# Strassen products of a two-layer graph network: sums read between the products, and quarter blocks for the output projection

## The chip, the cores and the metric

The kernel runs on one core of one Trainium2 chip. TensorE (PE) multiplies matrices, VectorE (DVE) and ScalarE (ACT) work elementwise and can read PE's results in PSUM, GpSimd (POOL) works elementwise on SBUF alone, and SyncE (SP) issues most of the DMAs. Each engine works through its own queue in order, and waits for others by semaphores. The metric is the device time of one execution in microseconds, the median of several runs. All data are 32-bit floats.

## The reference

x is 64 batches of 256 tokens with 512 features. Two layers follow each other, each with a layer norm and a ReLU ahead of it and a residual around it:

```
h = relu(layernorm(x));  x = x + (adj @ h) @ W0 + b0
h = relu(layernorm(x));  q, k, v = h @ Wq + bq, h @ Wk + bk, h @ Wv + bv     # 8 heads of 64
a = softmax(q k^T / 8 + (1 - adj) * -1e9)
x = x + (a v) @ Wo + bo
```

## The kernel before, in words

**Tiling.** The batches are worked in NG = 32 groups of two. All groups go through layer 0 first (`layer0`, L643), which leaves the residual and the turned hidden state in HBM; then all go through layer 1. Layer 1 of a group is: queries and keys (`queries_keys`, L755), scores (`score`, L825, in two halves of the heads, qd), values (`values`, L780), attention (`attend`, L860) and the output projection (`post`, L800). The loop at L970 interleaves neighbours: attend(g, 0), score(g, 1), queries and keys of g + 1, attend(g, 1), score(g + 1, 0), values of g + 1, output projection of g.

**Projections.** Every projection is a product of a 512x512 weight with 512 columns (two batches of 256 tokens), cut into 2x2 blocks of 256, and computed by Winograd's form of Strassen's algorithm: seven block products instead of eight. Their operands are sums of blocks: s1 to s4 of the weight, made once (`weight_sums`, L405), and t1 to t4 of the data (`Halves.sums`, L433), made by POOL for each group. `product` (L439) writes one block product into a PSUM bank with four matmuls, each 128 columns of weights by 256. There are eight banks; `bank` (L246) takes the one that has been free longest, and `give` returns it. Some products add up in the same bank: `project` (L447) writes a11 b11 into bank a, has it read, adds s2 t2 on top, has it read again, adds s3 t3, and so on; it uses four banks a, b, c and d. ACT (for q, k and v) or DVE (layer 0 and o, onto the residual x) reads a bank, and DVE adds the other parts (`add`, L608).

**Quarter size.** From group FIRST2 = 4 on, q, k and v use `project2` (L561). There four of the seven products (a11 b11, s1 t1, s2 t2, s3 t3) are done as before, and the three that are used in one place only (a12 b21, s4 b22, a22 t4) are cut once more into seven products of quarter blocks, one 128x128x128 matmul each (`product2`, L534). Of these seven, three go straight to their place in the bank `own`, and the four common ones (a11 b11, s2 t2, s3 t3, s1 t1) lie side by side in four quarters of another bank, `shared`. After all seven DVE adds each to the quarters that need it (`finish2`, L547): widths 512, 512, 384, 256 and 128 or 256. The output projection uses `project` for all groups.

**Order.** The order of the instructions is written by hand. PE's work is emitted in steps (a `yield` after each product), and after each step `tick` (L263) emits what was put off with `after(delay, ...)`: subtractions of the scores' bound (POOL, L846), exponents (ACT, L851), sums over keys (POOL, L858), divisions (DVE, L901), data sums. Each engine then runs its own instructions in this order.

**The end.** In the last group there is nothing left to project ahead, so the output projection of the group before (`run(post(g - 1))`, L989) stands between score and attend; then the last attention, and the last output projection (L1001), into which a check on the softmax's denominators (L1004 to L1011) is put.

Of the kernel before, what the change touches and what calls it, by code (L numbers as in the profile page):

```python
# [13 lines left out]
P = 128  # L14
# [184 lines left out]
def kernel(  # L199
# [247 lines left out]
    def project(s, halves, by_token, name, read, finish, in_place=False):  # L447

        def new(n):
            return bank([P, 2, N], f"{name}{n}")

        def p1():
            o["a"] = new("a")
            product(o["a"], s, "a11", halves, "b11", by_token, stop=False)
            o["u1"] = read(o["a"], 1)

        def p2():
            pb = new("b")  # L460
            product(pb, s, "a12", halves, "b21", by_token)
            finish(pb, o["u1"], 0, 0)
            give(pb)

        def p3():
            product(o["c"], s, "s4", halves, "b22", by_token, start=False)
            finish(o["c"], o["u2"], 0, 1)
            give(o["c"])

        def p4():  # L470
            pd = new("d")
            product(pd, s, "a22", halves, "t4", by_token)
            finish(pd, o.get("u3"), 1, 0)
            give(pd)

        def p5():
            o["c"] = new("c")
            product(o["c"], s, "s1", halves, "t1", by_token, stop=False)
            o["c22"] = read(o["c"], 0)

        def p6():
            product(o["a"], s, "s2", halves, "t2", by_token, start=False, stop=False)
            o["u2"] = read(o["a"], 2)

        def p7():
            product(o["a"], s, "s3", halves, "t3", by_token, start=False)
            o["u3"] = read(o["a"], 3)
            finish(o["a"], o["c22"], 1, 1)
            give(o["a"])

        o = {}
        for step in (p1, p5, p2, p6, p4, p7, p3) if in_place else (p1, p2, p6, p5, p7, p4, p3):
            step()
            yield

# [5 lines left out]
    FIRST2 = 4  # L501
    W2, spare = {}, []

    def block_sums(n):

        todo = []
        for a in ONCE:
            w = W[n][a]
            def part(i, j):
                return w[:, j, i * P:(i + 1) * P]  # L510
            s1, s2, s3, s4 = (spare.pop(0) for _ in range(4))
            W2[n, a] = dict(a11=part(0, 0), a12=part(0, 1), a22=part(1, 1), s1=s1, s2=s2, s3=s3, s4=s4)
            for o, p, q, op in ((s1, part(1, 0), part(1, 1), ALU.add), (s2, s1, part(0, 0), ALU.subtract),
                                (s3, part(0, 0), part(1, 0), ALU.subtract), (s4, part(0, 1), s2, ALU.subtract)):
                todo.append((nc.gpsimd.tensor_tensor, o, p, q, op))
        return todo
# [17 lines left out]
    def product2(own, shared, s, x, by_token, fresh):  # L534

        q = own.rearrange("p m (n k) -> p (m n) k", k=P)
        c11, c12, c21, c22 = (q[:, i, :] for i in ((0, 2, 1, 3) if by_token else (0, 1, 2, 3)))
        for o, a, b, start in ((shared[:, 0, :], "a11", "b11", True), (shared[:, 1, :], "s2", "t2", False),
                               (shared[:, 2, :], "s3", "t3", False),
                               (c22 if fresh else shared[:, 3, :], "s1", "t1", fresh),  # L540
                               (c11, "a12", "b21", False), (c12, "s4", "b22", False), (c21, "a22", "t4", False)):
            lhs, rhs = s[a], x.operand(b)
            if by_token:
                lhs, rhs = rhs, lhs
            nc.tensor.matmul(o, lhs, rhs, start=start, stop=True, skip_group_check=True)

    def finish2(o, own, shared, u, by_token, fresh):  # L547

        def quarters(t):
            return t.rearrange("p m (n k) -> p (m n) k", k=P)  # L550

        def spread(i, n):
            return shared[:, i:i + 1, :].to_broadcast([P, n, P])
        q = quarters(o)
        lower = q[:, 1::2, :] if by_token else q[:, 2:4, :]
        right = q[:, 2:4, :] if by_token else q[:, 1::2, :]
        return [(o, own, u), (q, spread(0, 4), q), (q[:, 1:4, :], spread(1, 3), q[:, 1:4, :]),
                (lower, spread(2, 2), lower),
                (right[:, 0, :], quarters(own)[:, 3, :], right[:, 0, :]) if fresh else (right, spread(3, 2), right)]

    def project2(n, halves, blocks, by_token, name, read, target):  # L561

        s = W[n]

        def new(i):
            return bank([P, 2, N], f"{name}{i}")

        def once(own, a, i, k, u, fresh):
            shared = bank([P, 4, P], f"{name}r")
            product2(own, shared, W2[n, a], blocks[ONCE[a]], by_token, fresh)  # L570
            return own, shared, finish2(target(i, k), own, shared, u, by_token, fresh)

        def finish_all(*products):
            for ops in zip(*(ops for _, _, ops in products)):
                for op in ops:
                    add(*op)
            for own, shared, _ in products:
                give(own)
                give(shared)

        pa = new("a")
        product(pa, s, "a11", halves, "b11", by_token, stop=False)
        u1 = read(pa, 1)
        yield
        pc = new("c")
        product(pc, s, "s1", halves, "t1", by_token, stop=False)
        c22 = read(pc, 0)
        yield
        product(pa, s, "s2", halves, "t2", by_token, start=False, stop=False)
        u2 = read(pa, 2)  # L590
        yield
        c12 = once(pc, "s4", 0, 1, u2, False)
        yield
        c11 = once(new("b"), "a12", 0, 0, u1, True)
        finish_all(c12, c11)
        yield
        product(pa, s, "s3", halves, "t3", by_token, start=False)
        u3 = read(pa, 3)
        add(target(1, 1), pa, c22)
        give(pa)  # L600
        yield
        finish_all(once(new("d"), "a22", 1, 0, u3, True))
        yield

    def partial(name, n):
        return tmp.tile([P, 2, N], F32, tag="u", name=f"u{n}_{name}")
# [4 lines left out]

    RESIDUAL = {0: (1, 1), 1: (0, 0), 2: (0, 1), 3: (1, 0)}
# [30 lines left out]
    def layer0(g):  # L643
# [17 lines left out]
        for d in range(DC):  # L661
# [5 lines left out]
            if d >= 2:  # L667
                halves.sums(nc.gpsimd, ("t1", "t2"), d - 2)
            if d == 3:
                halves.sums(nc.gpsimd, ("t3", "t4"))  # L670
# [7 lines left out]

        def read(ps, n):
            o = quarter(xt, *RESIDUAL[n])  # L680
            add(o, ps, o)
# [20 lines left out]
        def finish(ps, u, i, k):  # L702
            o = quarter(xt, i, k)
            add(o, ps, o)
# [15 lines left out]
        yield from project(W["0"], halves, True, f"w_{g}", read, finish)  # L720
# [14 lines left out]
    def hidden_sums(g, *steps):  # L735

        HH[g] = Halves(f"h_{g}", [H1T[g][:, k] for k in range(GB)], 0 if g else 1)
        for step, n in zip(steps, ("t1", "t2", "t3", "t4")):
            after(step, HH[g].sums, nc.gpsimd, (n,))

    H2 = {}

    def block_hidden(g, step):
# [3 lines left out]
        x = H1T[g][:, :, 2:4, :].rearrange("p k c (n j) -> p k c n j", j=P)  # L747
        both = Blocks(x, t)
        last = Blocks(HH[g].t["t4"].rearrange("p c (n j) -> p c n j", j=P), t4)
        H2[g] = {f"b2{k + 1}": Blocks(x[:, k], t[:, k]) for k in range(GB)}  # L750
        H2[g]["t4"] = last
        after(step, both.sums, nc.gpsimd)
        after(step + 1, last.sums, nc.gpsimd)

    def queries_keys(g):  # L755

        for n, store in (("q", Q), ("k", K)):
# [3 lines left out]
            def read(ps, m):  # L761
                u = partial(f"{n}_{g}", m)
                for c in range(2):
                    f = 2 * (m in (0, 3)) + c
                    nc.scalar.activation(u[:, c, :], ps[:, c, :], AF.Identity, bias=bias[:, f:f + 1])
                return u

            def target(i, k):
                o = store[g][i, k] = act.tile([P, 2, N], F32, tag=f"{n}{i}{k}", name=f"{n}_{g}_{i}{k}")
                return o  # L770

            def finish(ps, u, i, k):
                add(target(i, k), ps, u)

            if g < FIRST2:
                yield from project(W[n], HH[g], False, f"{n}_{g}", read, finish)
            else:
                yield from project2(n, HH[g], H2[g], False, f"{n}_{g}", read, target)

    def values(g):  # L780
# [3 lines left out]
        def read(ps, m):  # L784
            u = partial(f"v_{g}", m)
            nc.scalar.copy(u, ps)
            return u

        def finish(ps, u, i, k):
            add(V[g][i, k], ps, u)  # L790

        if g < FIRST2:
            yield from project(W["v"], HH.pop(g), True, f"v_{g}", read, finish)
# [253 lines left out]
```

## Time and profile before

| | |
|---|---|
| runs | 2690.47, 2687.57, 2688.24 us; median 2688.24 |
| profiled execution | 2688.09 us, its span 2686.3 us, mean granted clock 0.998 |
| layer 0 | about 0 to 641 us, 19.0 us a group |
| layer 1 | about 641 to 2686 us; one group, 1405.84 to 1469.33: 63.49 us, in which PE is busy 63.49, DVE 47.66, ACT 19.25, POOL 47.55 |
| end, 2640 to 2686.3 | PE busy 33.0 of 46.3 us, granted clock 0.91 |

Waits of PE, from the list of waits (who waits for whom, us in total, times, longest):

```profile
PE pa L323 <- DVE adj_p L318: 9.8, 1, 9.8
PE pf L1009 <- DVE worst L1007: 3.8, 1, 3.8
PE o_30a L444 <- POOL t_o L437: 2.8, 1, 2.8
PE q_1a L444 <- POOL t_h L437: 2.4, 1, 2.4
PE py L655 <- DVE adjT L325: 0.9, 1, 0.9
PE o_31b L444 <- DVE oT L901: 0.8, 1, 0.8
```

Nearly all of PE's waiting is at the start, at the change of layers and at the end. A row of the timeline has the start and the length in us, engine, line, operation, out<-in by the program's names, shape, count, and in brackets the idle time before with what ended it. A 32-bit matmul stands as two rows (passes), each with its weight load (PEld).

Widths and mean times of DVE's additions in one quarter-size projection, from the group rows of 1421.5 to 1428 (us busy, mean ns):

```profile
L609 DVE TENSOR_TENSOR v<-v_12r,v 128x512 f32<-128x512 f32 x3 | 2.0, 685 | 0.0
L609 DVE TENSOR_TENSOR v<-v_12r,v 128x256 f32<-128x256 f32 x3 | 1.1, 416 | 0.0
L609 DVE TENSOR_TENSOR v<-v_12r,v 128x384 f32<-128x384 f32 x2 | 1.0, 549 | 0.0
L609 DVE TENSOR_TENSOR v<-v_12b,v 128x128 f32<-128x128 f32 x1 | 0.3, 282 | 0.0
```

Additions that follow each other overlap: seven of them (512, 512, 384, 384, 256, 256, 256) take 3.20 us together, that is starts 0.598, 0.464 and 0.331 us apart.

### The profile page before, as it was taken

The page shows a single profiled execution, that of the slowest core. Times are in us where ns is not written, and L with a number is a line of the kernel's source. Part 1 is how long each engine was busy: PE and PEld are TensorE (multiplying, and loading weights), DVE is VectorE, ACT ScalarE, POOL GpSimd, SP SyncE. Part 2 cuts the span into 40 slices and gives each one's busy share as a digit, 9 for nine tenths or more (in the row PEclk, how much of TensorE's full clock was granted, in tenths as well). Part 3 has the DMA queues.
Part 4 walks back from the last instruction along what each step waited for, and adds up shares of the span by engine and source line. Part 5 has one row for each costly group of instructions (what it writes and reads, how often), then busy time and mean ns, then how long its engine had stood idle before and what let it go on. Part 6 is the DMA issues. An engine that isn't in the chain of part 4 may idle for free.

```text
span 2686.3 us, 47911 instructions
## 1 busy us (share of the span) xinstructions
PE 2659.3 (99%) x18684; PEld 2267.5 (84%) x18684; DVE 1958.6 (73%) x3789; ACT 868.9 (32%) x1537; POOL 1960.1 (73%) x1630
## 2 busy tenths in 40 slices
PE   8999999999999999999999999999999999999998
PEld 7888888888788888888888888888888888888886
DVE  7878787875455777777777777777777777777776
ACT  3444344443222233332222233222222333332222
POOL 6777777674777777777777777777777777777775
PEclk9999999999999999999999999999999999999999
DMA  7776666663112221111111111111122211111110
GB/s 188 187 198 162 163 170 166 164 157 97 31 54 61 55 52 48 48 48 48 48 48 48 48 48 48 48 48 48 56 63 63 56 48 48 48 48 48 48 48 33
DMA packets 281047, 210.80 MB, mean 78 GB/s; under 512 B 145904, under 2 KB 212976, under 8 KB 280816
## 3 DMA queue, kind: packets, MB, share of 16 engines
q1 hardware_dynamic: 280352, 207.15, 29.7%
q8 instruction: 150, 2.46, 0.4%
q10 hardware_dynamic: 464, 0.52, 0.1%
q14 instruction: 81, 0.66, 0.1%
HBM read 106.96 MB, written 100.66 MB: 77 GB/s over the span
## 4 chain that ended last, share of the span: by engine, by line
PE 97%; DVE 1%; POOL 1%; DMA 0%; issue 0%; SPq 0%; ACTq 0%; POOLq 0%; DVEq 0%
PE sc L835 8%; PE py L655 8%; PE pav L874 8%; PE pden L867 2%; POOL a L846 1%; DVE v L609 0%; DVE k L609 0%; PE v_29a L444 0%; PE q_29a L444 0%; PE v_28a L444 0%; PE v_27a L444 0%; PE v_25a L444 0%; PE q_25a L444 0%; PE v_24a L444 0%; PE q_23a L444 0%; PE q_21a L444 0%
## 5 line engine op out<-in xcount | busy, mean ns | idle before, releaser
L846 POOL TENSOR_TENSOR a<-a,top 128x1024 f32<-128x1024 f32 x254 | 593.2, 2369 | 512.3 <-DVE a L840 512.3
L840 DVE SCALAR_TENSOR_TENSOR a<-sc,maskT 128x512 f32<-128x512 f32 x512 | 312.0, 682 | 58.1 <-PE sc L835 57.4
L858 POOL TENSOR_TENSOR as<-a 128x512 f32<-128x512 f32 x256 | 319.2, 1281 | 0.7 <-DVE r L691 0.7
L851 ACT ACTIVATE a<-a 128x1024 f32<-128x1024 f32 x256 | 264.1, 1054 | 22.4 <-POOL a L846 22.4
L885 DVE RECIPROCAL den<-den 128x128 f32<-128x128 f32 x256 | 223.7, 919 | 38.0 <-ACT den L881 37.9
L835 PE MATMUL sc<-q,k 64*128 64x256 f32 x2048 | 239.2, 383 | 0.6 <-DVE a L840 0.6
L835 PEld LDWEIGHTS sc<-q,k 64*128 64x128 f32 x2048 | 194.3, 187 | 46.1 <-issue 26.3
L874 PE MATMUL pav<-a,v 128*32 128x256 f32 x4096 | 232.7, 379 | 0.0
L655 PE MATMUL py<-adjT,h 128*128 128x256 f32 x1024 | 228.2, 381 | 0.9 <-DVE adjT L325 0.9
L655 PEld LDWEIGHTS py<-adjT,h 128*128 128x128 f32 x1024 | 195.7, 191 | 28.5 <-ACT h L630 1.2
L874 PEld LDWEIGHTS pav<-a,v 128*32 128x32 f32 x4096 | 133.1, 110 | 87.9
L685 ACT ACTIVATE h<-x,nb,rs 128x512 f32<-128x512 f32 x128 | 97.1, 806 | 318.3 <-POOL nb L54 318.1
L881 ACT ACTIVATE den<-pden 128x512 f32<-128x512 f32 x64 | 38.2, 597 | 493.8 <-PE pden L867 493.1
L53 POOL TENSOR_TENSOR rs<-rs,mhalf 128x2 f32<-128x2 f32 (+1 forms) x97 | 78.8, 812 | 123.7 <-DVE nb L52 123.7
L978 POOL TENSOR_TENSOR x<-x,bo_r 128x512 f32<-128x512 f32 x128 | 159.4, 1277 | 12.2 <-DVE x L609 12.2
L634 POOL TENSOR_TENSOR x<-x,b_r 128x512 f32<-128x512 f32 x128 | 159.1, 1276 | 1.0 <-ACT h L630 0.9
L437 POOL TENSOR_TENSOR t_y<-yT,t_y 128x256 f32<-128x256 f32 (+1 forms) x96 | 87.3, 909 | 41.2 <-ACT yT L665 38.6
L706 DVE BATCH_NORM_STATS2 st<-x 128x6 f32<-128x256 f32 x256 | 96.4, 418 | 4.4
L630 ACT ACTIVATE h<-x,nb,rs 128x512 f32<-128x512 f32 x128 | 93.9, 805 | 10.8 <-POOL nb L54 10.8
L42 DVE BATCH_NORM_STATS2 st<-x 128x6 f32<-128x512 f32 x128 | 85.6, 669 | 7.5 <-DMA x<-in_x_dram 7.5
L437 POOL TENSOR_TENSOR t_y<-yT 128x256 f32<-128x256 f32 (+1 forms) x96 | 88.0, 916 | 2.3 <-ACT yT L665 0.9
L691 DVE STREAM_TRANSPOSE r<-h 128x512 f32<-128x512 f32 x128 | 82.7, 683 | 2.1 <-ACT h L685 1.4
(5610 smaller groups left out, 6381.4 us busy)
## 6 DMA issues: line engine op xcount, KB each, us to landing
x<-in_x_dram SPq DMA_DIRECT2D x256, 128.0 KB, 3.5
residual<-x SPq DMA_DIRECT2D x256, 128.0 KB, 2.3
hidden<-r SPq DMA_DIRECT2D x128, 256.0 KB, 4.6
h1T<-hidden SPq DMA_DIRECT2D x64, 512.0 KB, 9.4
x<-residual SPq DMA_DIRECT2D x32, 1024.0 KB, 6.7
out_dram<-x SPq DMA_DIRECT2D x62, 512.0 KB, 3.2
w_sb<-in_L_gnn_weight_dram SPq DMA_DIRECT2D x1, 1024.0 KB, 6.5
wq_sb<-in_L_gnn_Wq_dram SPq DMA_DIRECT2D x1, 1024.0 KB, 7.7
```

What stands on the lines that cost most here:

```text
L437: eng.tensor_tensor(self.t[n][:, c, :], self.operand(p, c), self.operand(q, c), op=ALU.subtract)
L634: nc.gpsimd.tensor_tensor(xt[:, t, :], xt[:, t, :], b0_r, op=ALU.add)
L655: nc.tensor.matmul(pss[d][:, b * N:(b + 1) * N], h[:, b * NT + k, d * P:(d + 1) * P], adjT[:, k, :], start=(k == 0), stop=(k == NT - 1))
L685: nc.scalar.activation(h1[:, k * NT + t, :], xt[:, k * NT + t, :], AF.Relu, bias=nb[:, t:t + 1], scale=rs[:, t:t + 1])
L835: nc.tensor.matmul(ps[j][:, kt * N:(kt + 1) * N], k[j * HD:(j + 1) * HD, c, kt * P:(kt + 1) * P], q[j * HD:(j + 1) * HD, c, :], start=True ...
L840: nc.vector.scalar_tensor_tensor(a[:, j * NT:(j + 1) * NT, :].rearrange("p k n -> p (k n)"), ps[j], SCALE, maskT_f, op0=ALU.mult, op1=ALU.add)
L846: nc.gpsimd.tensor_tensor(a, a, top_b, op=ALU.subtract)
L851: nc.scalar.activation(a, a, AF.Exp)
L858: nc.gpsimd.tensor_tensor(AS[c, b], a4[:, :, 0, :], a4[:, :, 1, :], op=ALU.add)
L874: nc.tensor.matmul(po[f][h * 32:(h + 1) * 32, b * N:(b + 1) * N], v[:, k, h * HD + f * 32:h * HD + f * 32 + 32], A[h // 2, b][:, (h % 2) * ...
L885: nc.vector.reciprocal(rden[:, c * P:(c + 1) * P], den[:, c * P:(c + 1) * P])
L978: after(9 + t, lambda t, xt: nc.gpsimd.tensor_tensor(xt[:, t, :], xt[:, t, :], L1["o"][1], op=ALU.add), t, X[g])
```

## The change

- `project` uses three banks: a, c and b. Its order is now a11 b11 (a), s3 t3 (c), s2 t2 (a), a12 b21 (b), s1 t1 (a), a22 t4 (c), s4 b22 (a). After each product the bank's running sum is read into the place where it is wanted, and there are seven reads in place of eight. The first read into a place (`first`) is ACT's for q, k and v; the places are the final tiles, with no tiles between.
- `project2` is written anew, likewise in order. The products a12 b21 (p2, bank pb) and a22 t4 (p4, bank pc) share a bank px for their common sums: each has one quarter in which a11 b11, s2 t2 and s1 t1 are added up, with a read after each, and one for s3 t3. s4 b22 (p3) goes into bank pa, with its common sums in a bank py.
- The order of the data sums follows: t3 is needed by the second product.
- The output projection uses `project2` too, and all four projections use it from group 2 on (FIRST2 = 2). POOL makes the block sums of its data (`block_outputs`; the last group on DVE) and those of Wo; s3 of the block sums is made in place.
- Exponents of one score are put off by 3, 4, 5 and 8 (or 6) steps in place of 3, 4, 5 and 6.
- In the last group, five of the seven steps of the output projection before stand ahead of the last attention and two behind it; the bias additions come 5 steps earlier, and the division is not put off by 8 steps.

```diff
+    def project(s, halves, by_token, name, place, first, done=None):
...
+        pa = bank([P, 2, N], f"{name}a")
+        product(pa, s, "a11", halves, "b11", by_token, stop=False)
+        put(pa, 0, 0)
+        yield
+        pc = bank([P, 2, N], f"{name}c")
+        product(pc, s, "s3", halves, "t3", by_token, stop=False)
+        put(pc, 1, 1)
+        yield
+        product(pa, s, "s2", halves, "t2", by_token, start=False, stop=False)
+        put(pa, 1, 0)
+        yield
+        pb = bank([P, 2, N], f"{name}b")
+        product(pb, s, "a12", halves, "b21", by_token)
+        more(pb, 0, 0)
...
+        product(pa, s, "s1", halves, "t1", by_token, start=False, stop=False)
+        more(pa, 1, 1)
...
+        product(pc, s, "a22", halves, "t4", by_token, start=False)
+        more(pc, 1, 0)
...
+        product(pa, s, "s4", halves, "b22", by_token, start=False)
+        put(pa, 0, 1)
...
-    FIRST2 = 4
+    FIRST2 = 2
...
+        pb, px = bank([P, 2, N], f"{name}b"), bank([P, 4, P], f"{name}x")
+        p2 = Inner("a12", 0, 0, pb, px[:, 0:2, :], True)
+        p4 = Inner("a22", 1, 0, pc, px[:, 2:4, :], False)
+        p2.u1(True)
+        p2.add(p2.sum, 0, 0)
+        for i, k in ((0, 0), (0, 1), (1, 0)):
+            p2.only(i, k)
+        p4.u1(False)
+        p4.add(p4.sum, 0, 0)
+        p4.only(0, 0)
+        yield
+        product(pa, s, "s1", halves, "t1", by_token, start=False, stop=False)
+        more(pa, 1, 1)
+        complete(1, 1)
+        yield
+        py = bank([P, 2, P], f"{name}y")
+        p3 = Inner("s4", 0, 1, pa, py, False)
...
+        p3.u1(True)
+        if add_up:
+            p3.add(p3.sum, 0, 0)
+        else:
+            begin(p3.sum, 0, 0)
+            begin(part(pa, 1, 1), 1, 1)
+        p4.only(0, 1)
+        p4.only(1, 0)
+        for p in (p2, p4):
+            p.u2()
+            p.add(p.sum, 1, 0)
+            p.s3t3()
+            p.add(p.r, 1, None)
+        yield
+        p3.only(1, 0)
+        p3.only(0, 0)
+        p3.only(0, 1)
+        if not add_up:
+            begin(part(pa, 1, 0), 1, 0)
+            begin(part(pa, 0, 1), 0, 1)
+        p3.u2()
+        p3.add(p3.sum, 1, 0)
+        if add_up:
+            more(pa, 0, 1)
+        else:
+            p3.add(part(pa, 0, 0), 0, 0)
+        give(pa)
...
+            add(o[:, m, 0:n], u[:, m, 0:n], o[:, m, 0:n])
+        give(pb)
+        more(pc, 1, 0)
+        give(pc)
+        for p in (p2, p4):
+            p.u3()
+            p.add(p.sum, None, 1)
+        give(px)
+        complete(0, 0)
+        complete(1, 0)
+        p3.s3t3()
+        p3.add(p3.r, 1, None)
+        p3.u3()
+        p3.add(p3.sum, None, 1)
+        give(py)
...
-            if d >= 2:
-                halves.sums(nc.gpsimd, ("t1", "t2"), d - 2)
+            halves.sums(nc.gpsimd, ("t1",) if d < 2 else ("t3", "t2"), d % 2)
             if d == 3:
-                halves.sums(nc.gpsimd, ("t3", "t4"))
+                halves.sums(nc.gpsimd, ("t4",))
...
-        yield from project(W["o"], halves, True, f"o_{g}", read, finish, in_place=True)
+        if g < FIRST2:
+            yield from project(W["o"], halves, True, f"o_{g}", place, add_to, done)
+        else:
+            yield from project2("o", halves, O2.pop(g), True, f"o_{g}", place, add_to, done, add_up=True)
...
-                after(3 + 2 * c + b, exponent, a)
+                after((3, 4, 5, 8 if sum_delay > 3 else 6)[2 * c + b], exponent, a)
...
-            run(post(g - 1))
+            last = post(g - 1)
+            run(last, 5)
         attend(g, 1)
...
     tick()
+    run(last)
     last = post(NG - 1)
     run(last, 4)
```

In `Inner`, `mm` is one 128x128x128 matmul; `u1`, `u2` and `u3` add a11 b11, s2 t2 and s1 t1 to the running sum, `s3t3` writes the other quarter, `only` the three products with a place of their own, and `add` is a DVE addition of a quarter of the bank, or of two joined, to one or two quarters of the target.

## The prediction

> **What bounds the kernel now.** I read the page first: the busy line, and the chain of work that ended last.
>
> ```profile
> PE 2659.3 (99%) x18684; PEld 2267.5 (84%) x18684; DVE 1958.6 (73%) x3789; ACT 868.9 (32%) x1537; POOL 1960.1 (73%) x1630
> ...
> PE 97%; DVE 1%; POOL 1%; DMA 0%; issue 0%; SPq 0%; ACTq 0%; POOLq 0%; DVEq 0%
> ```
>
> TensorE (PE) is never out of work: whatever lengthens its own row lengthens the kernel, and DVE and POOL have a quarter of their time spare. Then the timelines of PE and DVE in one quarter-size projection (v of group 12: start, length, name).
>
> ```profile
> 1422.13 0.39 PE L545 MATMUL v_12b<-wv_sb,t 128*128 128x128 f32 x2
> 1422.36 1.89 PE L444 MATMUL v_12a<-wv_sb,t_h 128*128 128x256 f32 x8
> ...
> 1425.20 0.39 PE L545 MATMUL v_12d<-spare_adjT,t_h 128*128 128x128 f32 x2
> 1425.42 0.39 PE L545 MATMUL v_12d<-wv_sb,t 128*128 128x128 f32 x2
> ```
> ```profile
> 1422.56 0.69 DVE L609 TENSOR_TENSOR v<-v_12b,u_v 128x512 f32<-128x512 f32 x1 [0.80 <-PE v_12b L545]
> 1423.16 3.20 DVE L609 TENSOR_TENSOR v<-v_12r,v 128x512 f32<-128x512 f32 x7
> ```
>
> One f32 matmul is two passes (x2). A 128-wide one takes 0.223 us of PE (1425.20 to 1425.42), a 256-wide one 0.431 (eight passes in 1.727). DVE reads the sums 1 to 4 us after PE wrote them, and PE has gone on: nothing waits. The last views are of two places where PE did wait, and of the clock in windows round such waits (length; PE, PEld, DVE, ACT and POOL busy; clock).
>
> ```profile
> 2664.39 1.29 DVE L901 TENSOR_TENSOR oT<-pav,den 128x512 f32<-128x512 f32 x2
> ```
> ```profile
> 2665.13 0.30 PEld L444 LDWEIGHTS o_31b<-wo_sb,oT 128*128 128x128 f32 x2 [1.17 <-DVE oT L901]
> ```
> ```profile
> 681.11:684.53 3.42, 1.06 (x5) 0.96 (x6) 0.00 (x0) 2.38 (x6) 3.42 (x3) 1.00 0.00 0
> 684.53:687.94 3.41, 3.41 (x10) 2.49 (x9) 0.69 (x1) 1.65 (x3) 3.33 (x5) 0.50 0.02 5
> ...
> 2667.67:2671.08 3.41, 1.38 (x7) 0.88 (x5) 2.85 (x3) 0.00 (x0) 3.41 (x3) 1.00 0.00 0
> 2671.08:2674.50 3.42, 1.65 (x6) 1.35 (x7) 1.30 (x5) 0.00 (x0) 1.80 (x2) 0.50 0.22 77
> ```
>
> The first oT ends at 2665.08 and PE's weight load starts at 2665.13: a wait costs 0.054 us beyond the other engine's end, and the weights are loaded only then (that first matmul lasts 483 ns, not 379: 0.104 more). And where PE had worked only 1.06 or 1.38 us of 3.41, the next window's clock was 0.50.
>
> [...] 1.06 and 1.38 us of 3.41 fell, while 1.74 us in 2643.78:2647.19 did not. [...]
>
> **The change part by part.** Base: the profiled execution's 2688.09 us (span 2686.3), the median of the runs being 2688.24.
>
> (a) *Matmuls.* Quarter-size form has 16 256-wide and 21 128-wide matmuls: 16 x 0.431 + 21 x 0.223 = 11.58 us; half-size form 28 x 0.431 = 12.07. Saved 0.5 us in 36 projections (o in groups 2 to 31, q, k, v in groups 2 and 3; the built program has 324 more matmuls, which is 36 x 9): -18 us.
>
> (b) *Quarter-size sums.* Before, the four common sums of a product lie in four quarters of a bank, and are read after all are done. Now p2 and p4 share one bank (px) and each adds its sums up in one quarter, read between the products. In the built order, every matmul of `u2, s3t3` of p2 and then of p4 waits for the DVE addition just ahead of it. Prices: an unwaited 128-wide matmul's start to DVE's start is 0.425 us (the v_12b row at 1422.13, DVE at 1422.56); after a wait 0.104 more, 0.529. A DVE addition ends after 0.28 (128 wide), 0.416 (256), 0.549 (384), 0.69 (512), from the group rows; the next one starts 0.198, 0.331, 0.464, 0.598 after the start of the one before. DVE's end to PE's start 0.054.
>
> The chain for q, k, v, from the start of p2's u2:
> - u2 0; DVE 0.425 to 0.705; s3t3 0.759; DVE 1.288 to 1.704; p4's u2 1.758; DVE 2.287 to 2.567; p4's s3t3 2.621 (next matmul 0.327 later).
> - Three matmuls of p3 and its u2 follow at 2.95, 3.17, 3.40, 3.62, p2's u3 at 3.84. The second half of this stretch hangs on DVE's queue: ACT copies two quarters of pa (3.40 + 0.425 to 4.22, the second to 4.50; a 128-wide copy isn't in the trace; 256 wide takes 0.471, 512 wide 0.587, so 0.36 to 0.42, I take 0.39, and the ends move the chain by 0.03), and DVE adds in order 128 (4.24), 128 (4.53), 384 (4.73), 512 (5.20), and only then p2's u3 (5.79 to 6.21). p4's u3 waits for that: 6.26. s3t3 of p3 6.59, DVE 6.79 and 7.12 to 7.54, p3's u3 7.59, next product 7.92.
> - PE's own work in it is 12 x 0.223 = 2.68. Idle: 5.24 us. Nothing hides it, PE being in order and full. 90 projections: +472 us.
>
> In o there is no ACT copy, but DVE's queue before p2's u3 is 128, 512 (0.107 after the first's end, it adds to the same cells), 256, 128, 512: the same steps give 8.28, so 5.61; and p4's u1 waits 0.34 more, since DVE first adds the 512-wide quarter before it. 30 x 5.95 = +178 us.
>
> What DVE has besides (8 score additions of 0.6, four reciprocals of 0.83, two divisions of 0.6: 9.3 us) is queued ahead of a projection that follows an attention, and is done in the 13 us (8.2 of attention and scores, three products of 1.73) before the quarter-size part starts. The bounds: below, 3.7 us a projection if loads were still pulled ahead and DVE's queue empty; above, 6.5 with a division or score addition in front.
>
> (c) *Clock.* Of the 7.9 us chain PE works 2.7 us, so some of the windows in it [...] hold less than the limit of 1.4 to 1.7 us. Sliding a 3.41 us window along the times above, 2.2 to 4.0 us of start positions are under the limit: 0.6 to 1.2 windows a chain, each making a next window that is 0.8 to 0.95 full lose half its work. That is 1.0 to 1.4 us; I take 1.2. 120 chains: +144 us. Lower bound 0.
>
> (d) *Half-size order* (layer 0, groups 0 and 1). The same banks' reads lie one product (1.73 us) apart from the next write; a read needs 0.417 + 0.69 + 0.054 = 1.16, so PE does not wait; one read in eight falls away on DVE, off the path. But the second product now needs t3 instead of none: in group 29 POOL's third sum ends at 577.33, the second product would start at 577.22 (575.49 + 1.73), so 0.11 + 0.054 + 0.104 = 0.27 us, in 31 groups +8 us. Bounds 0 and 30.
>
> (e) *POOL, ACT, DMA.* Block sums of o: 4.3 us of POOL a group (1.27 + 0.73 + 0.73 + 0.73 + 0.46 + 0.46), on 47.6 of 63.5 us: hidden even in a group as short as before, and queued behind four subtractions of 2.37; if it came late, PE would wait at the fourth part of o. Exponent order: ACT is 19 of 63.5 us busy; nothing. SP's DMAs are the same ones, issued two or three products apart from before; the weight sums of o and the bias additions of the last group, moved on POOL, are under the same cover.
>
> (f) *Last group.* 2640 to 2686.3 has 13 us of PE idle and clock 0.91. Two products of the group before now fill the wait for the last attention. I take -5, and -2 for the earlier t2 of group 1 (its wait of 2.6 us at 683). Bounds -14 and +10.
>
> Sum: 2688.1 - 18 + 472 + 178 + 144 + 8 - 7 = 3465 us.
>
> **Rivals.**
> - *No clock drops* (waits as above, windows stay over the limit): 3465 - 144 = 3321. For it: no stall is longer than 2.2 us. Against: the two rows with 0.50 followed idle of 2.4 and 2.2 us in the window, and a chain has 5.2.
> - *More queue on DVE and longer slow windows*: one more 0.6 us addition in front in each chain and half a window more at half clock (0.7): 3465 + 120 x 1.3 = 3621. For it: the clock at the end stayed low for two windows, 2671 to 2678. Against: between chains PE is full for 9 us.
> - *The read is covered* (faster): the waits are there but PE doesn't feel them, and only (a) and (f) are left: 2688 - 25 = 2663. The same idea works at half size, where 1.16 us of turnaround lies under 1.73 of other products. Quarter size would need a turnaround under 0.22 us, or as much other work between; the built order has none between those four matmuls. It decides at that 0.22.
> - *The change doesn't do what it says*: 324 more matmuls and the waits are in the built program; excluded.
>
> **How the numbers follow.** The forecast 0.50, no clock drops 0.26, longer chains 0.16, covered 0.04; the rest, 0.04, lies between 2690 and 3260 (some waits cheaper than priced). The range 3260 to 3620 takes in the first three with their bounds, about 0.85. About 0.2% is what a measurement of this kernel can tell from no change. Slower 0.95, faster 0.04, same 0.01; one sign holds nearly all.
>
> **What would show it.** The profile after should have PE idle before the quarter-size matmuls, released by DVE's additions, some 5 us in each of 120 projections (top of the list of waits); in the timeline of one, DVE additions 0.86 and 1.0 us apart with single matmuls between, and a gap of 2 to 2.5 us before p4's u3; one layer-1 group near 90 us instead of 63.5; clock digits of 8 or 9 in layer 1 with many short windows at 0.50; layer 0 within 10 us of before. If PE stays at 99% busy and the waits list is short, (b) is wrong and the third rival holds; if the clock stays at 1.00, (c) is.

## The result, and the profile after

| | median us | runs (lowest to highest) | ratio to before, 95% interval |
|---|---|---|---|
| before | 2689.1 | 4 (2687.6 to 2690.5) | |
| changed kernel | 3504.2 | 4 (3502.3 to 3511.8) | 1.304 (1.301 to 1.306) |

The change makes the kernel 815 us slower; 3465 us was forecast, and the median lies in the range. The profiled execution took 3511.8 us (span 3510.0), the slowest of the four, so sums from its trace are some 8 us above the median.

The page after: busy time and instructions, granted clock in 40 slices, and shares of the chain that ended last.

```profile
PE 3000.2 (85%) x19332; PEld 2436.9 (69%) x19332; DVE 1889.4 (54%) x4096; ACT 910.8 (26%) x1747; POOL 2103.0 (60%) x1861
...
PEclk9999999999999999999999999989898989898988
...
PE 74%; DVE 16%; issue 4%; POOL 3%; ACT 3%; DMA 0%; DVEq 0%; SPq 0%; POOLq 0%
```

PE was 99% busy and is 85% busy. DVE is on the chain for 16% of the span, though its own busy time fell from 1959 to 1889 us: it is not overloaded, PE waits for its answers. PE's busy time rose by 341 us although it has 17 us less to do; matmuls at half clock are counted in it (in group 10's o two that follow each other start 0.43 us apart, at 1644.61 and 1645.04, instead of 0.22), and single matmuls with their run-out (a row of 0.39 us, where the next matmul starts after 0.22).

From here on a chain is the 12 quarter-size matmuls from p2's u2 to the end of a projection; there are 120. The chain in v of group 12 (PE's timeline, then DVE's):

```profile
1717.36 0.39 PE L553 MATMUL v_12x<-spare_w_s,t 128*128 128x128 f32 x2
1718.13 0.49 PE L553 MATMUL v_12x<-wv_sb,t 128*128 128x128 f32 x2 [0.38 <-DVE v L667]
1719.13 0.49 PE L553 MATMUL v_12x<-spare_w_s,t 128*128 128x128 f32 x2 [0.52 <-DVE v L667]
1720.00 0.49 PE L553 MATMUL v_12x<-wv_sb,t 128*128 128x128 f32 x2 [0.38 <-DVE v L667]
...
1721.22 0.39 PE L553 MATMUL v_12x<-spare_w_s,t 128*128 128x128 f32 x2
1723.43 0.49 PE L553 MATMUL v_12x<-spare_w_s,t 128*128 128x128 f32 x2 [1.83 <-DVE v L667]
1723.76 0.39 PE L553 MATMUL v_12y<-wv_s,t 128*128 128x128 f32 x2
1724.77 0.49 PE L553 MATMUL v_12y<-spare_w_s,t 128*128 128x128 f32 x2 [0.62 <-DVE v L667]
1725.09 1.25 PE L444 MATMUL o_11a<-wo_sb,oT 128*128 128x256 f32 x5
```
```profile
1717.78 0.29 DVE L667 TENSOR_TENSOR v<-v_12x,v 128x128 f32<-128x128 f32 x1 [0.20 <-PE v_12x L553]
1718.65 0.42 DVE L667 TENSOR_TENSOR v<-v_12x,v 128x256 f32<-128x256 f32 x1 [0.58 <-PE v_12x L553]
...
1721.90 0.55 DVE L667 TENSOR_TENSOR v<-v_12b,v 128x384 f32<-128x384 f32 x1
1722.37 0.68 DVE L667 TENSOR_TENSOR v<-v_12c,v 128x512 f32<-128x512 f32 x1
1722.96 0.41 DVE L667 TENSOR_TENSOR v<-v_12x,v 128x256 f32<-128x256 f32 x1
```

Two kinds of waiting are seen. In the first four rows PE and DVE take turns on bank px, one of them idle while the other works: 0.77, 1.00 and 0.87 us a turn for matmuls of 0.22. Then PE is ready with p4's u3 at 1721.44, but the addition that reads p2's u3 stands in DVE's queue behind those of banks pb and pc, and ends only at 1723.37. From u2 to the next product it is 7.73 us, of which 2.68 are PE's own (12 x 0.223).

For the whole kernel I took each matmul's start to the next one's start; what exceeds 0.216 us a pass (256 wide) or 0.112 (128 wide) is put to the wait before it, to the weight load after a wait, or to the clock:

| us of PE's row, profiled executions | before | after | difference |
|---|---|---|---|
| projections and adjacency at full speed | 2120.8 | 2103.6 | -17.2 |
| waits for DVE's additions in the chains | 0 | 583.8 | +583.8 |
| weight loads after a wait | 13.7 | 73.2 | +59.5 |
| half clock: projections | 4.2 | 122.0 | +117.8 |
| half clock: scores and attention (their whole time) | 520.4 | 585.1 | +64.7 |
| waits for POOL's t3 in layer 0 | 0 | 19.1 | +19.1 |
| the rest (start, change of layers, end) | 27.2 | 23.2 | -4 |

### The profile page after: what moved, and what is told of

Its sections match the earlier page's. It is cut to its first block, busy times and chain, and to the rows that moved or that the text cites. A ratio compares the mean times of both kernels' runs of the same rounds, so it can differ in the third digit from the quotient of the medians.

```text
span 3510.0 us, 49651 instructions
## 1 busy us (share of the span) xinstructions
PE 3000.2 (85%) x19332; PEld 2436.9 (69%) x19332; DVE 1889.4 (54%) x4096; ACT 910.8 (26%) x1747; POOL 2103.0 (60%) x1861
## 4 chain that ended last, share of the span: by engine, by line
PE 74%; DVE 16%; issue 4%; POOL 3%; ACT 3%; DMA 0%; DVEq 0%; SPq 0%; POOLq 0%
PE pav L931 7%; PE sc L892 7%; DVE x L667 5%; DVE k L667 3%; DVE q L667 3%; DVE v L667 3%; PE py L713 3%; PE pden L924 3%; POOL t_y L437 2%; ACT h L738 1%; DVE st L758 1%; ACT yT L723 0%; POOL rs L53 0%; DVE st L42 0%; ACT q L828 0%
## 5 line engine op out<-in xcount | busy, mean ns | idle before, releaser
L943 DVE RECIPROCAL rest<-rest 128x128 f32<-128x128 f32 x256 | 224.5, 921 | 117.6 <-ACT rest L939 117.6
L931 PE MATMUL pav<-a,v 128*32 128x256 f32 x4096 | 274.3, 427 | 0.0
L939 ACT ACTIVATE rest<-pden 128x512 f32<-128x512 f32 x64 | 38.2, 597 | 858.2 <-PE pden L924 858.2
L931 PEld LDWEIGHTS pav<-a,v 128*32 128x32 f32 x4096 | 150.3, 126 | 123.1 <-issue 48.4
L437 POOL TENSOR_TENSOR t_y<-yT 128x256 f32<-128x256 f32 x128 | 92.7, 729 | 47.5 <-ACT yT L723 44.2
L924 PE MATMUL pden<-as,ones 128*32 128x256 f32 x1024 | 95.3, 502 | 0.1
```

Of the source, the lines that this page charges most:

```text
L437: eng.tensor_tensor(self.t[n][:, c, :], self.operand(p, c), self.operand(q, c), op=ALU.subtract)
L924: nc.tensor.matmul(pd[h * 32:(h + 1) * 32, b * N:(b + 1) * N], ones[:, 0:32], AS[h // 2, b][:, h % 2, :], start=True, stop=True, tile_posi ...
L931: nc.tensor.matmul(po[f][h * 32:(h + 1) * 32, b * N:(b + 1) * N], v[:, k, h * HD + f * 32:h * HD + f * 32 + 32], A[h // 2, b][:, (h % 2) * ...
L943: nc.vector.reciprocal(rden[:, c * P:(c + 1) * P], den[:, c * P:(c + 1) * P])
```

## The experiments

Twelve kernels, in the order of the questions; ratios are to the kernel before on the same chip.

| kernel | median us (lowest to highest) | ratio, 95% interval |
|---|---|---|
| e1_half_only | 2750.2 (2748.6 to 2751.8) | 1.023 (1.021 to 1.025) |
| e3_fill | 3342.9 (3342.6 to 3343.5) | 1.243 (1.241 to 1.245) |
| g1_fill_hidden | 3343.2 (3341.5 to 3344.7) | 1.243 (1.241 to 1.245) |
| e4_dve_order | 3299.6 (3295.6 to 3303.5) | 1.228 (1.226 to 1.230) |
| f3_two_banks | 3150.7 (3138.9 to 3162.8) | 1.170 (1.167 to 1.174) |
| f4_two_banks_order | 2925.7 (2925.1 to 2925.7) | 1.088 (1.086 to 1.090) |
| e5_apart | 2763.8 (2763.1 to 2764.1) | 1.028 (1.026 to 1.030) |
| f7_apart_seam | 2735.9 (2735.5 to 2737.7) | 1.018 (1.016 to 1.019) |
| e6_half_order | 2733.5 (2732.5 to 2734.8) | 1.017 (1.015 to 1.018) |
| f1_before_last | 2689.3 (2688.1 to 2690.7) | 1.000 (0.999 to 1.001) |
| f5_last_pool | 2683.9 (2682.3 to 2685.1) | 0.998 (0.997 to 0.999) |
| f6_last_first2 | 2679.9 (2679.6 to 2681.4) | 0.997 (0.996 to 0.998) |

### Is it the quarter-size sums?

e1_half_only: every projection of layer 1 at half size, with the three banks, and no block sums (q and k shown; the same line is changed for v and o).

```diff
-            if g < FIRST2:
+            if g < NG:
                 yield from project(W[n], HH[g], False, f"{n}_{g}", place, first)
```

> The changed kernel, with all projections of layer 1 in half-size form (three banks, the new order), so without any quarter-size part; the block sums of data and weights are left out, since nothing reads them. Theory (the quarter-size sums make PE wait): 2688 before, +42 for the 84 projections q, k, v of groups 4 to 31 that lose the 0.5 us of the quarter form, +21 for the t3 wait in layer 0, -7 at the end: about 2744 us, clock above 0.99. Rival (the new half-size order or the new order of the last group costs a good part of the 815 us): above 2900.

2750 us. The three banks read between half-size products cost next to nothing; all but 61 of the 815 us come with the quarter-size part. Of these 61, 40 are the matmuls that half size has more (2161.1 us at full speed against 2120.8 before), 19 are in layer 0 (below).

### What is the clock's share?

e3_fill and g1_fill_hidden put extra 128-wide matmuls of operands at hand into a bank that nobody reads, 17 and 12 in each chain (shown is g1):

```diff
             p.u2()
             p.add(p.sum, 1, 0)
+            fill(1)
             p.s3t3()
...
             p.add(p.sum, None, 1)
+            if p is p2:
+                fill(6)
```

> The changed kernel with 17 more 128-wide matmuls in each quarter-size part (120 parts, 455 us of PE work in all), put where PE waits for DVE: 2 in each of the first three gaps, 8 before p4's s1 t1, 3 before p3's; they write a bank of their own that nothing reads. Theory (about 187 us of the loss is the half clock that the idle of the waits brings): the waits stay, the clock goes back to 0.99 or more, the time falls to about 3320 us although PE has more to do. Rival (the half clock has another cause, or costs little): 3504 or more, up to 3960 if the added matmuls don't fit into the waits.

> The changed kernel with 12 filler matmuls (128 wide, of operands at hand, into a bank of their own) in each of the 120 chains, in the places where TensorE waits for VectorE and shorter than the waits there: 1, 2 and 1 in the three first waits, 6 in the wait ahead of p4's u3, 2 ahead of p3's u3; 322 us of TensorE work that no wait should get longer by. Theory [...] only the clock's share of 187 us goes: 3317 us. Rival (idle gaps themselves make the clock fall, whatever the work in the window): 3504 or more.

Both take 3343 us: 161 us *less* than the changed kernel, with 455 and 322 us more for PE to do. In g1 the chain of v of group 12 goes from 1658.10 to 1665.84, 7.74 us against 7.73; over the whole trace the waits in the chains shrink by some 319 us, where the extra matmuls take 322. So the waits are as long as before and only filled; the mean clock is 0.998, where it was 0.933, and scores and attention take 520.0 us again. Why was g1's number missed by 26 us? 187 is the share in the profiled execution, 8 us of which the median does not have; 4 us of it are slow windows that the kernel before has too; and filling adds some 7 us of weight loads after a wait. The last 7 us stay open (e3 missed by 23 us). The clock's share is 161 us and up to about 180.

In the changed kernel's trace the granted clock, on record from 16.2 us on, is 1.00 or 0.50, and it changes on a grid of 3.41 us. A view by the windows of this grid (length; PE, PEld, DVE, ACT, POOL busy with their passes or instructions; clock) shows where it falls:

```profile
1627.33:1630.74 3.41, 1.19 (x7) 1.00 (x8) 2.30 (x6) 0.75 (x1) 3.17 (x6) 1.00 0.00 0
1630.74:1634.16 3.42, 3.42 (x10) 2.72 (x9) 0.44 (x2) 0.00 (x0) 3.42 (x4) 0.50 0.02 5
...
1640.98:1644.40 3.42, 2.14 (x14) 1.57 (x13) 1.90 (x5) 0.00 (x0) 3.19 (x5) 1.00 0.00 0
1644.40:1647.81 3.41, 2.55 (x12) 2.26 (x11) 1.64 (x4) 0.00 (x0) 0.65 (x2) 0.50 0.00 0
1647.81:1651.22 3.41, 1.61 (x6) 1.32 (x6) 2.08 (x6) 0.00 (x0) 0.00 (x0) 0.50 0.00 0
1651.22:1654.64 3.42, 3.42 (x34) 1.59 (x37) 0.72 (x2) 0.69 (x2) 0.00 (x0) 0.50 0.86 301
1654.64:1658.05 3.41, 3.41 (x62) 1.93 (x55) 1.47 (x2) 0.00 (x0) 0.00 (x0) 1.00 0.99 324
```

The first pair is the case that I had priced: a window with little work, one slow window, then full speed. The other is not: the two windows that follow inside the same chain have 12 and 6 passes at 0.50, and the clock is still 0.50 in the third, in the attention. Of the 77 slow stretches 28 last three windows, 46 one; 138 windows in all.

PE's busy share does not tell after which window the clock is 0.50 (before, it was 1.00 after a window with 1.74 us, here 0.50 after one with 2.14), for a single matmul's run-out counts as busy. The passes in it tell more, counted at 0.112 or 0.216 us each. Counted so, the 77 windows of the changed kernel ahead of a fall hold at most 1.38 us of 3.41, and the windows at full clock with full clock after them at least 1.32. Windows at half clock with another behind them hold up to 1.32, and those ahead of a return, two aside, at least 1.62. Passes that straddle an edge of a window can be counted in more than one way, which moves these figures by 0.1 to 0.2 us. In g1 the chain of v of group 12 has 24 matmuls (12 of them extra), 5.35 us of passes in 7.74 us, where the changed kernel has 2.68 in 7.73.

### Is it DVE's order, the shared bank, or the number of reads?

e4_dve_order moves DVE's additions of pb and pc behind the last sums:

```diff
-            add(o[:, m, 0:n], u[:, m, 0:n], o[:, m, 0:n])
-        give(pb)
-        more(pc, 1, 0)
-        give(pc)
         for p in (p2, p4):
             p.u3()
...
         p3.add(p3.sum, None, 1)
         give(py)
+            add(o[:, m, 0:n], u[:, m, 0:n], o[:, m, 0:n])
+        give(pb)
+        more(pc, 1, 0)
+        give(pc)
```

> The changed kernel with DVE's additions of the banks pb and pc put behind the last sums of the quarter-size part instead of between p3's second sum and p2's third. Theory (the 2 us wait before p4's s1 t1 is DVE's queue): 1.06 us less in q, k, v, 1.12 in o, so 128 us less waiting, and some 30 to 50 us less at half clock: about 3340 us. Rival (the wait is the turnaround of the two engines): within 10 us of 3504.

3300 us, 205 less: 132 us of waiting (584 to 452) and the rest clock (mean 0.961 in the profiled execution, 0.933 in the changed kernel), of which more went than I had expected. f3_two_banks leaves the reads as they are, gives p2 and p4 a bank each and lets their matmuls alternate:

```diff
-        pb, px = bank([P, 2, N], f"{name}b"), bank([P, 4, P], f"{name}x")
+        pb, px, pz = bank([P, 2, N], f"{name}b"), bank([P, 2, P], f"{name}x"), bank([P, 2, P], f"{name}z")
...
-        p4.u1(False)
+        p4.u1(True)
...
         for p in (p2, p4):
             p.u2()
             p.add(p.sum, 1, 0)
+        for p in (p2, p4):
             p.s3t3()
             p.add(p.r, 1, None)
```

> The changed kernel with a bank each for the common sums of p2 and p4 and their matmuls interleaved (u2, u2, s3t3, s3t3); running sums, reads and matmul counts are the same. Theory (a matmul waits for the read of its bank, so what counts is which reads stand between two uses of a bank): the three waits of 0.54, 0.78 and 0.58 us become one of about 0.4, and p4's u3 no longer waits for the read of p2's u3; p3's u3 still waits for DVE's queue. Chain idle 3.0 instead of 5.2 us, 264 us less in 120 chains, and fewer windows at half clock, some 95 us less: about 3145 us. Rival (each read between two products has a fixed price, whatever bank it is in): about 3504, at most 50 less.

f4_two_banks_order does both.

> As the kernel with two banks, and DVE's additions of banks pb and pc moved behind the last sums. Theory: chain idle about 1.8 us instead of 5.2 (410 us less), and nearly no window under the clock's limit (165 us less): about 2930 us. Rival (additions moved back delay the next projection's banks by as much): about 3145, as with two banks alone.

3151 us (two runs near 3139, two near 3162) and 2926 us, where 3145 and 2930 were expected; the waits in the chains fall from 584 to 316 and 187 us. The chain of v of group 12 in f4, the same 12 matmuls:

```profile
1513.62 0.39 PE L553 MATMUL v_12x<-spare_w_s,t 128*128 128x128 f32 x2
1513.85 0.39 PE L553 MATMUL v_12z<-spare_w_s,t 128*128 128x128 f32 x2
1514.39 0.49 PE L553 MATMUL v_12x<-wv_sb,t 128*128 128x128 f32 x2 [0.16 <-DVE v L669]
1514.72 0.39 PE L553 MATMUL v_12z<-wv_sb,t 128*128 128x128 f32 x2
...
1516.06 0.39 PE L553 MATMUL v_12z<-spare_w_s,t 128*128 128x128 f32 x2
1516.46 0.49 PE L553 MATMUL v_12y<-wv_s,t 128*128 128x128 f32 x2
1517.65 0.49 PE L553 MATMUL v_12y<-spare_w_s,t 128*128 128x128 f32 x2 [0.70 <-DVE v L669]
```

It takes 4.35 us to the next product (at 1517.97) instead of 7.73. Two banks and the order of DVE's additions are worth 578 of the 815 us, with not one read less. The rival that each read has a fixed price is out. The second bank and the alternation were not tried apart, and each bank holds one tile, so these runs do not tell whether PE's wait goes by the bank or by the tile.

### The sums kept apart: is all well then?

e5_apart keeps the changed kernel but for the quarter-size part, where the common sums lie in four quarters and are read after all seven matmuls, as before; for all four projections.

> The changed kernel with the quarter-size part as it was before the change (the four common sums side by side in a bank, read after all seven), for q, k, v and o from group 2 on; half-size order, block sums and last group as in the changed kernel. Theory (only the sums read in between cost time, the rest of the change is worth its matmuls): 2688 - 18 + 21 - 7 = 2684 us, PE busy 98 to 99 percent. Rival (the quarter form of the output projection costs more on DVE and POOL than it saves on PE): above 2720.

2764 us, 80 more than the theory says, which so holds only in part. From the list of waits:

```profile
PE o_6a L444 <- DVE x L626: 1.3, 1, 1.3
PE o_2a L444 <- DVE x L626: 1.2, 1, 1.2
```

So in all groups; 46.9 us with the load after the wait. At the seam from v to o, DVE still has v's last additions to do when o's first product is ready to be read. Only one product (1.73 us) lies between that and the next matmul into the same bank; the kernel before has two. In both kernels DVE starts on o's first product 4.00 us after that product starts (median of groups 4 to 29). Group 11, whose first product starts at 1425.65 before and at 1459.51 in e5:

```profile
1429.65 0.68 DVE L609 TENSOR_TENSOR x<-o_11a,x 128x512 f32<-128x512 f32 x1
1430.83 1.89 PE L444 MATMUL o_11a<-wo_s,t_o 128*128 128x256 f32 x8
```
```profile
1463.51 0.68 DVE L626 TENSOR_TENSOR x<-o_11a,x 128x512 f32<-128x512 f32 x1
1464.34 1.97 PE L444 MATMUL o_11a<-wo_s,t_o 128*128 128x256 f32 x8 [1.21 <-DVE x L626]
```

So DVE is no later there than before; the order of the products has lost its cover. f7_apart_seam takes o's a12 b21 third:

```diff
+        c11 = once(new("b"), "a12", 0, 0, True) if add_up else None
+        if add_up:
+            yield
         product(pa, s, "s2", halves, "t2", by_token, start=False, stop=False)
```

> The kernel with the sums kept apart and the output projection at quarter size too (2764 us), with one step moved in the output projection alone: a12 b21 stands third, so that two products instead of one lie between the first read of bank a and the next matmul into it. Theory (VectorE comes late to that read, by 1.2 us more than one product covers, 30 times): 45 us less, about 2719. Rival (VectorE stays behind, and the wait moves to a later product or the scores): about 2755.

2736 us: 28 less, not 45. The wait at bank a is gone (46.9 to 3.4 us), but scores take 265.6 us instead of 252.1 (235.3 before), waiting for DVE again:

```profile
PE sc L855 <- DVE a L860: 5.1, 29, 0.6
```

Both theories hold by half. With o at quarter size DVE has more to do: in a group of e5 (1436.42 to 1500.36) it is busy 52.21 of 63.94 us, against 47.66 of 63.49 before. This shows behind o: DVE's last addition of o ends 5.0 us after PE's last matmul of o starts in e5 and 5.6 us in f7, against 1.1 us before, and the additions for the scores stand behind it in DVE's queue. The 0.5 us that o saves on PE was not gained in either of the two orders; one in which DVE has the time was not tried.

### Layer 0 and the last group

e6_half_order is e1_half_only with a12 b21 second and s2 t2 third, so that t3 is wanted only by the fourth product.

> The kernel with every projection of layer 1 at half size (2750 us), its products in another order with the same three banks: a11 b11 (a), a12 b21 (b), s2 t2 (a), s3 t3 (c), s1 t1 (a), a22 t4 (c), s4 b22 (a), so that the first data sum of layer 0 is wanted by the third product and not the second. Theory (the waits of layer 0 for POOL come from t3 wanted as second): 19 us less, 2731. Rival (POOL is late by as much with t2 for the third product): 2750.

2733.5 us, 16.7 less. The wait is for t3. POOL and PE in group 10 of the changed kernel:

```profile
225.48 1.27 POOL L413 TENSOR_TENSOR wk_sb<-wk_sb 128x512 f32<-128x512 f32 x1
226.71 0.73 POOL L437 TENSOR_TENSOR t_y<-yT 128x256 f32<-128x256 f32 x1
227.39 0.73 POOL L437 TENSOR_TENSOR t_y<-yT,t_y 128x256 f32<-128x256 f32 x1
228.08 0.73 POOL L437 TENSOR_TENSOR t_y<-yT 128x256 f32<-128x256 f32 x1
```
```profile
228.87 0.48 PE L444 MATMUL w_10c<-w_sb,t_y 128*128 128x256 f32 x1 [0.68 <-POOL t_y L437]
```

From group 4 to 19 POOL also makes the sums of layer 1's weights (L413), 1.27 us ahead of t3. The second product now wants t3, where before the first product to want a data sum was the third. In group 29, on which I had priced this, there is no such work and no wait.

f1_before_last is the kernel before with the changed last group alone.

> The kernel before with the changed kernel's last group alone (five of the seven steps of the output projection before ahead of the last attention, two behind it, the division not put off, bias additions and sums over keys earlier). Theory (the term of -5 us is right): 2684 us. Rival (the wait comes back later in the last group): 2689, within 2 us of the kernel before.

2689.3 us, no difference. The end from o_30 on is 41.0 us long instead of 46.2, as hoped, but PE waits ahead of it:

```profile
PE pden L867 <- POOL as L858: 5.7, 3, 3.4
```

POOL's sums over keys for attend(31, 0) now stand behind a subtraction (2.4 us) that was DVE's and behind data sums of o_30 that came later. f5_last_pool gives the subtraction back to DVE and puts those sums behind the last key sum (against f1_before_last):

```diff
-                if (g, qd) == (NG - 1, 1) and c + b == 2:
+                if g == NG - 1 and c + b == 2:
...
-                after(5, HO[g].sums, nc.gpsimd, ("t2", "t3", "t4"))
+                after(7, HO[g].sums, nc.gpsimd, ("t2", "t3", "t4"))
```

> The kernel before with the changed last group, but two things of it left as they were or put later, so that GpSimd's sums over keys for the last group's first attention are not queued behind them: one subtraction of the scores' bound stays on VectorE, and the data sums of the output projection before come after the last sum over keys. Theory (the 5 us gained in the last group were lost again in 4.7 us of waiting for these sums): 2684 us. Rival (the wait comes back elsewhere): 2689.

f6_last_first2 has quarter size from group 2 on as well (six projections more).

> As the one with the mended last group, and quarter size for q, k and v from group 2 on instead of 4, with the block sums of the weights at the changed kernel's times. Theory (six projections with 0.5 us less on TensorE each): 3 us less than that one, 2681. Rival (block sums of the weights come late on GpSimd): 2684 or more.

2683.9 and 2679.9 us; the wait is down to 1.7 us. The last is faster than both kernels, by 0.33% (ratio 0.9967, 0.9955 to 0.9979).

## Why the prediction was right, and where it was not

- *(a) Matmuls, -18:* right; -17.2.
- *(b) Quarter-size sums, +650:* right; 583.8 of waits and 59.5 of weight loads, 643. The links came as worked out: 0.77, 1.77, 2.64, 3.86 and 6.07 us from u2 in v of group 12, where 0.76, 1.76, 2.62, 3.84 and 6.26 were predicted, and 7.73 for the next product instead of 7.92 (at full clock q takes 7.97, k 8.06 and o 8.35, where 7.92 and 8.28 were predicted). The prices came from three things in the trace of before: a matmul's start to DVE's (0.425 us), DVE's end to PE's start (0.054), and the queue on DVE in its order. That a matmul also waits for a read of another part of its bank was my assumption; no view of before shows it. f3 and f4 show the mechanism by taking parts of it away. In the changed kernel p4's u3 starts at 1723.43, 0.06 us after the read of another quarter of px ends and 2.21 after p2's u3; in f4, with a bank each, 0.22 after p2's u3 (1515.84 and 1516.06).
- *(c) Clock, +144:* that the waits bring half clock was right (in g1, with the waits filled, the mean clock is 0.998 instead of 0.933), the size too small: 182 us in the profiled execution, 161 to 180 in the median. I had let each underfull window cost one slow window. Drops are at the low end of the 0.6 to 1.2 a chain that I had counted (77 in 120 chains, 0.64), but inside a chain a slow window can be followed by another (1644.40 and 1647.81, with 12 and 6 passes), and 28 stretches go on for three: 138 slow windows at 1.3 us each, 1.15 a chain. There is a slip in the sum as well: 0.6 to 1.2 windows that lose half of 0.8 to 0.95 of 3.41 us make 0.8 to 1.9 us a chain, not 1.0 to 1.4. The limit that I took, a busy time between 1.4 and 1.7 us, was an estimate from the windows of before with 1.06, 1.38 and 1.74 us (clock after them 0.50, 0.50 and 1.00). The 2.14 us in the changed kernel, with 0.50 after it, lie outside it; the count of passes is the better measure there. The waits in that window, 1640.98 to 1644.40, are only 0.38, 0.52 and 0.38 us.
- *(d) Layer 0, +8:* the mechanism was right, the place wrong: 19.1 us, not 0.27 us in every group but 0.7 us of idle (0.83 from start to start) in sixteen (from 4 to 19, where POOL has weight sums, without 14, and in 30) and 4.5 in the first. A row taken from one group was made to stand for all. Layer 0 was to stay within 10 us of before; its group 30 starts 24 us later (618.5 instead of 594.5), as behind the first group's wait two windows (26.48 to 33.31) are at 0.50.
- *(e) POOL, ACT, DMA, nothing:* not refuted in the changed kernel. But I did not ask what DVE's time would be if PE did not wait. e5 and f7, without reads between the quarter-size products, stop at 2764 and 2736 us: the first for want of a second product at the seam, both because DVE ends o's additions late and the scores wait. So the rival "the read is covered", at 2663, left out a cost; whether another order reaches it is not shown.
- *(f) Last group, -7:* wrong as a step of its own (f1: nothing). The 5 us were there and were lost to POOL's queue, past which two things had been moved; f5 shows both halves. In the changed kernel itself the waits in the chain of v_31 hide this: no wait for these sums stands in its list.

Sum for the profiled execution, by its span: 2686.3 - 17.2 + 643.3 + 182.5 + 19.1 - 4 = 3510.0. The forecast was 47 us below its time of 3511.8: 38 us from (c), 11 from (d) and 3 from (f) and what is left, 1 from (a), less 7 from (b) (39 us below the median).

## What to carry to other kernels

A running sum that is read between its products cost next to nothing here where the work between two uses of the bank was longer than the turn from PE to DVE and back: an estimated 1.16 us (0.417 + 0.69 + 0.054, from the rows of before) under a product of 1.73 (with nothing ahead of the read in DVE's queue; at the seam in e5 a product of 1.73 us was too little). At a quarter of the size the turn was still 0.77 to 1.0 us, and the work 0.22. Where such turns can't be avoided, give each chain a bank of its own and interleave the chains, and keep long additions out of DVE's queue ahead of the ones that PE waits for. When waits appear, count the passes in the windows in which the profile's clock changes (3.41 us here), slow windows included; and when a step is moved past a queue, look at the groups in which that queue carries something else.

## What the runs showed of the hardware

- In the changed kernel's trace the granted clock was 0.50 in 138 windows of 3.41 us, in 77 stretches, and its mean 0.933. The windows ahead of a fall held at most 1.38 us of matmul passes, the other windows at full clock at least 1.32 (give or take 0.1 to 0.2 by how edges are counted).
- Extra matmuls in the waits made the kernel 161 us faster: 3343 us with 12 or 17 of them in a chain (mean clock 0.998), 3504 with none (0.933).
- A matmul that waited for DVE had its weights loaded only after the wait (in v of group 12 the load and the matmul both start at 1723.43), and took 0.49 us instead of 0.39; in 120 chains this made 60 us.
